# One block of rows fewer, and the last shared expert woven with the return of the routed rows

## The chip, the cores and the metric

The kernel runs on one core of a Trainium2 chip. The metric is the device time of one execution in microseconds (us). A core has five engines that run side by side, each with its own in-order stream of instructions: TensorE (PE, matrix products; its weight loads are shown as PEld), VectorE (DVE), ScalarE (ACT), GpSimd (POOL) and SyncE (SP, which only issues transfers here). Transfers between the device memory and the on-chip buffers run on 16 DMA engines and are issued by SP, ACT or POOL; an indirect transfer, whose rows are picked by a list of row numbers, is issued by POOL.

## The reference

The program is a two-layer decoder on 4 batches of 512 tokens with 512 features. Layer one has causal attention, cross attention and a ternary feed-forward network; layer two has attention, a learned adjacency and a mixture of experts. Only the last part is touched by the change:

```python
logits = flat @ router_w.T                       # 2048 tokens, 16 experts
scores = softmax(logits)
_, topk_idx = top_k(logits + router_bias, 2)     # two experts for each token
... # their scores, divided by the sum of the two, become combine[n, e]
for e in range(16):
    h = silu(flat @ Wu[e]) * (flat @ Wg[e])      # 512 -> 256
    out = out + combine[:, e:e+1] * (h @ Wd[e])  # 256 -> 512
out = out + silu(flat @ Su) * (flat @ Sg) @ Sd   # shared expert, 512 -> 512 -> 512
x = layernorm(x + out)
```

Each token so goes to two routed experts, and each token also goes through the shared expert.

## The kernel before, in words

All of it is in `experts`. The 4096 pairs of a token and an expert are sorted by expert into rows of a list `xs` in device memory, in blocks of 128 rows that belong to one expert each. Since each expert's last block may be partly empty, the list can need at most `NB = (2*B*S + NE*(P-1)) // P` blocks, which is 47. The blocks are worked on in three interleaved streams (`NS = 3`) of `LS = 16` blocks, and 3 x 16 is `NBP = 48`, so that the kernel before works on 48.

The order of the work, as the text has it:

1. POOL sends the rows of all 16 tiles of 128 tokens into `xs` (L1294, 32 indirect transfers, two for each tile).
2. `shared(b, acc[b])` is run for the batches 0, 1 and 2 while the rows travel. It goes through the shared expert in two halves of 256 hidden features. In each half, there are two products of `xT` with `swu` and `swg` (L1193, 8 matmuls for each of two groups of 128 features), a Silu on ACT (L1198), a multiplication on DVE into `sh` (L1199), and then two products with `swd` (L1204, 8 matmuls each), which DVE adds to the sum (L1210).
3. The 48 blocks. For each, SP loads the expert's weights where they differ from the last ones of its stream, and the 128 rows into `xb` (L1329). PE transposes them (L1334), DVE copies the result (L1336), PE multiplies (L1339, 8 matmuls), ACT and DVE make `h` (L1344, L1346), PE transposes `h` (L1349) and multiplies by `wd` (L1353, 4 matmuls), ACT copies the result into `yb` (L1358) and issues its store into the list `ys` in device memory (L1359). The tags `xb` and `yb` have three buffers each (`bufs=3` of the pool `hp`).
4. `shared(B - 1, acc[B - 1])`, the shared expert of the last batch.
5. The return. For each of 16 tiles of tokens, and each of its two experts, POOL gathers 128 rows of `ys` into a buffer `yg` (L1366), and DVE multiplies them by the token's weight and adds them to the sum (L1370). `yg` has four buffers of its own, which are called homes here. After the four tiles of a batch comes `layernorm(b, acc[b])`: statistics on DVE (L105, L106), a square root on ACT (L108), a reciprocal (L110) and four scalings on DVE (L112). Then SP stores the batch (L1375).

A gather needs every store into `ys` to have landed, since any row may lie in any block. The sum of the last batch (`acc[3]`, which is `X[3]`, shown as `x` in the profile) can take no routed rows before both halves of its shared expert have been added by L1210.

The text of the kernel is not the order in which an engine runs. The framework's planner lays down a fixed stream for each engine before anything runs: it simulates the program and gives an engine the earliest instruction of the text among those that are ready by its own estimate. In the trace, the statistics of batch 0 stand between multiplications of L1370 that the text has ahead of them, and L1199 of the last batch stands between multiplications that the text has behind it. On the chip, each stream is then kept to, even where the instruction at its head waits and the one behind it could run.

Of the kernel before, what the change touches and what calls it, by code (L numbers as in the profile page):

```python
# [13 lines left out]
F32 = mybir.dt.float32  # L14
# [7 lines left out]
P = 128  # L22
B, S, D = 4, 512, 512
# [17 lines left out]
def decoder_kernel(ctx: ExitStack, tc: tile.TileContext, a: dict, out: bass.AP):  # L41
# [16 lines left out]
    def psum_pair():  # L58
        return ps["sc"].tile([P, 2, 512], F32, tag="sc", name="sc")

    def psum_tp(dt=F32, n=4):
        return ps["tp"].tile([P, n, P], dt, tag="tp", name="tp")

    def psum_mm():
        return ps["mm"].tile([P, 512], F32, tag="mm", name="mm")
# [25 lines left out]
    for b in range(B):  # L91
        xb = const.tile([P, NT, D], F32, tag=f"x{b}", name=f"x{b}")
# [1002 lines left out]
    NB = (2 * B * S + NE * (P - 1)) // P  # L1095
    NS = 3
    LS = -(-NB // NS)
    NBP = NS * LS

    def experts(xs, ys):  # L1100
        with tc.tile_pool(name="mx", bufs=1) as xp:

            acc = [
                xp.tile([P, NT, D], F32, tag=f"acc{b}", name=f"acc{b}") for b in range(2)
            ] + X[2:]
# [78 lines left out]
            def shared(b, acc):  # L1184

                for half in range(2):
                    h = xp.tile([P, F // P, S], F32, tag="sh", name="sh", bufs=2)
                    for f in range(F // P):
                        col = ts(half * (F // P) + f, P)
                        pp = psum_pair()  # L1190
                        for j, w in enumerate((swu, swg)):
                            for c in range(NK):
                                T.matmul(  # L1193
                                    pp[:, j, :], w[:, c, col], xT[b][:, c, :],
                                    start=(c == 0), stop=(c == NK - 1),
                                )
                        s = xp.tile([P, S], F32, tag="ss", name="ss", bufs=2)
                        A.activation(s, pp[:, 0, :], AF.Silu)  # L1198
                        V.tensor_tensor(h[:, f, :], pp[:, 1, :], s, ALU.mult)  # L1199
                    for k in range(NT // 2):  # L1200
                        po = psum_pair()
                        for i in range(2):
                            for f in range(F // P):
                                T.matmul(  # L1204
                                    po[:, i, :], h[:, f, ts(2 * k + i, P)],
                                    swd[:, half * (F // P) + f, :],
                                    start=(f == 0), stop=(f == F // P - 1),
                                )
                        two = slice(2 * k, 2 * k + 2)
                        V.tensor_tensor(  # L1210
                            acc[:, two, :], po, (acc if half else X[b])[:, two, :], ALU.add
                        )

            with tc.tile_pool(name="sims3", bufs=1) as sp, tc.tile_pool(name="adj", bufs=2) as ap:
                sims = Similarities(sp)
# [6 lines left out]
                rest = sp.tile([P, 1], F32, tag="rest", name="rest")  # L1222
                V.tensor_scalar(rest, gam, -1.0, 2.0, ALU.mult, ALU.add)
                for b in range(B):
                    mix_adjacency(b, sims, ap, half, rest)
                    t = xp.tile([P, NK, S], F32, tag=f"xT{b}", name=f"xT{b}")
# [64 lines left out]
            for t in chain(range(2 * NT, TT), range(2 * NT)):  # L1291
                b, i = divmod(t, NT)
# [6 lines left out]
                        tc.declare_no_dep(d.ins, e.ins, reason="rows of their own")  # L1299
                    sent.append(d)  # L1300
            for b in range(3):
                shared(b, acc[b])

            with tc.tile_pool(name="mw", bufs=1) as wp, tc.tile_pool(name="mh", bufs=3) as hp:
                wug = [wp.tile([P, NK, 2, F], F32, tag=f"wug{s}", name=f"wug{s}") for s in range(NS)]
                wd = [wp.tile([P, F // P, D], F32, tag=f"wd{s}", name=f"wd{s}") for s in range(NS)]
                last = None
                for k in range(LS):
                    for s in range(NS):
                        j = s * LS + k  # L1310

                        with tc.issue_after(last.ins) if last else nullcontext():
                            e = nc.sync.value_load(ebi[0:1, j : j + 1], min_val=0, max_val=NE - 1)
                            kw = {}
                            if k:
                                kw["cond"] = nc.sync.value_load(
                                    newi[0:1, j : j + 1], min_val=0, max_val=1
                                )
                        for q, n in enumerate("ug"):
                            nc.sync.dma_start(  # L1320
                                wug[s][:, :, q, :],
                                a["W" + n][bass.ds(e, 1)].rearrange("o (c p) f -> p (o c) f", p=P),
                                **kw,
                            )
                        last = nc.sync.dma_start(
                            wd[s], a["Wd"][bass.ds(e, 1)].rearrange("o (c p) f -> p (o c) f", p=P), **kw
                        )
                        xb = hp.tile([P, D], F32, tag="xb", name="xb")
                        d = nc.sync.dma_start(xb, xs[ts(j, P), :])  # L1329
                        for e in sent:  # L1330
                            tc.add_manual_dep(d.ins, e.ins.name, SYNC, reason="all rows are there")
                        tp = psum_tp()
                        for c in range(NK):
                            T.transpose(tp[:, c, :], xb[:, ts(c, P)], ident)  # L1334
                        xbT = hp.tile([P, NK, P], F32, tag="xbT", name="xbT")
                        V.tensor_copy(xbT, tp)  # L1336
                        pp = psum_pair()
                        for c in range(NK):
                            T.matmul(  # L1339
                                pp[:, 0, :], xbT[:, c, :], wug[s][:, c, :, :].rearrange("p q f -> p (q f)"),  # L1340
                                start=(c == 0), stop=(c == NK - 1),
                            )
                        sl = hp.tile([P, F], F32, tag="sl", name="sl")
                        A.activation(sl, pp[:, 0, :F], AF.Silu)  # L1344
                        h = hp.tile([P, F], F32, tag="h", name="h")
                        V.tensor_tensor(h, pp[:, 0, F:], sl, ALU.mult)  # L1346
                        th = psum_mm()
                        for c in range(F // P):
                            T.transpose(th[:, ts(c, P)], h[:, ts(c, P)], ident)  # L1349
                        hT = hp.tile([P, F // P, P], F32, tag="hT", name="hT")  # L1350
                        A.copy(hT, th[:, :F].rearrange("p (c t) -> p c t", t=P))
                        for c in range(F // P):
                            T.matmul(  # L1353
                                pp[:, 1, :], hT[:, c, :], wd[s][:, c, :],
                                start=(c == 0), stop=(c == F // P - 1),
                            )
                        yb = hp.tile([P, D], F32, tag="yb", name="yb")
                        A.copy(yb, pp[:, 1, :])  # L1358
                        nc.scalar.dma_start(ys[ts(j, P), :], yb)  # L1359
                shared(B - 1, acc[B - 1])  # L1360
                for b in range(B):
                    for i in range(NT):
                        t = b * NT + i
                        for k in range(2):
                            y = hp.tile([P, D], F32, tag="yg", name="yg", bufs=4)
                            G.indirect_dma_start(  # L1366
                                out=y, out_offset=None, in_=ys,
                                in_offset=bass.IndirectOffsetOnAxis(pos[k][:, t : t + 1], 0),
                            )
                            V.scalar_tensor_tensor(  # L1370
                                acc[b][:, i, :], y, wt[k][:, t : t + 1], acc[b][:, i, :],
                                ALU.mult, ALU.add,
                            )
                    layernorm(b, acc[b])
                    nc.sync.dma_start(out[b].rearrange("(t p) d -> p t d", p=P), acc[b])  # L1375

    xs = tc.dram_tile([NBP * P, D], F32, name="xs")
    ys = tc.dram_tile([NBP * P, D], F32, name="ys")


    def selecting(batches, pool, before=()):
# [43 lines left out]
    with psum(2, 2, 2):  # L1425
        experts(xs, ys)
# [47 lines left out]
```

## Time and profile before

| what | us |
|---|---|
| median of 3 runs | 2590.51 (2584.24 to 2602.18) |
| profiled execution, its own time | 2586.26 |
| span of that execution, first to last instruction | 2584.5 |
| first expert product of the blocks (L1339) on the chain | at 2189.58 |
| issue of the last store into `ys` (L1359) | at 2511.56 |
| first and last issue of a gather (L1366) | at 2514.38 and 2570.67 |
| issue of the last batch's store (L1375) | at 2579.1 |

The columns of the page's groups are: line, engine, operation, output and inputs, count, then the busy time and the mean of one in ns, then how long the engine sat idle just ahead of them and what ended most of that. PE's mean in such a group is longer than its pace, since its matmuls overlap. Over the whole program, PE is busy for 88% of the span, DVE for 56%, ACT for 44%, POOL for 24%. These shares say little for the change, which touches the last 75 us alone: from 2514.4 to the end, a stretch of 70.10 us, PE is busy for 38.97 us, DVE for 48.79, ACT for 9.99 and POOL for 33.35.

### The profile page before, as it was taken

To read this page: it belongs to the slowest core of one execution; us is meant where nothing else is said; L and a number is where in the kernel's file an instruction comes from. 1 tells how busy PE (TensorE), PEld (TensorE's weight loads), DVE (VectorE), ACT (ScalarE), POOL (GpSimd) and SP (SyncE) were. 2 spreads that over 40 slices of the span, in tenths; PEclk is the share of its full clock that TensorE was granted. 3 is DMA by queue.
4 is the path that set the end of the run, shared out by engine and by line. 5 is a ranking of instruction groups with operands and counts; after the bars stand their busy time and mean duration, and the time that the engine had idled before them with its cause. 6 is when DMAs were issued, how large, how long until landed. Compare 5 with 4: busy or idle time off the path is not lost. (4 is left out here: it accounts for less than half of the span.)

```text
span 2584.5 us, 34904 instructions
## 1 busy us (share of the span) xinstructions
PE 2284.4 (88%) x13080; PEld 1010.3 (39%) x13080; DVE 1437.7 (56%) x3146; ACT 1128.1 (44%) x1770; POOL 624.9 (24%) x1218
## 2 busy tenths in 40 slices
PE   6899999979899899998995899989985999999995
PEld 2334333423333333355553334434342334444442
DVE  2455455567878788578886355545554672111117
ACT  0632462326777677656663443282331430221211
POOL 7300120033334233066674310040000004000004
PEclk9999999889999999999998999989987999999997
DMA  6500000072412210000001100000001006534535
GB/s 217 149 22 1 1 1 1 1 265 94 130 34 91 74 34 17 1 1 1 1 1 32 52 1 1 1 1 1 1 3 58 9 1 231 164 106 157 173 118 183
DMA packets 89884, 156.93 MB, mean 61 GB/s; under 512 B 7152, under 2 KB 39280, under 8 KB 89712
## 3 DMA queue, kind: packets, MB, share of 16 engines
q1 hardware_dynamic: 72304, 115.86, 13.9%
q10 hardware_dynamic: 12288, 22.03, 2.3%
q0 software_dynamic: 5120, 16.78, 2.0%
q8 instruction: 103, 1.69, 0.3%
q14 instruction: 69, 0.57, 0.1%
HBM read 161.99 MB, written 47.71 MB: 81 GB/s over the span
## 5 line engine op out<-in xcount | busy, mean ns | idle before, releaser
L552 DVE TENSOR_REDUCE nm<-sc 128x2 f32<-128x1024 f32 x256 | 304.2, 1218 | 99.7 <-PE sc L422 99.1
L590 ACT ACTIVATE p<-sc 128x1024 f32<-128x1024 f32 x256 | 248.5, 1024 | 135.3 <-PE sc L422 135.3
L246 DVE CUSTOM_DVE_ANT_0 e<-sc,late_keys 128x256 bf16<-128x256 f32 (+3 forms) x512 | 222.8, 484 | 130.9 <-PE sc L422 130.7
L296 ACT ACTIVATE p<-sc 128x512 f32<-128x512 f32 (+3 forms) x256 | 165.9, 700 | 234.1 <-PE sc L422 233.9
L422 PE MATMUL mm<-p,va 128*32 128x512 f32 (+3 forms) x2048 | 217.4, 529 | 0.4 <-ACT oT L605 0.3
L1339 PE MATMUL sc<-wug,xbT 128*128 128x512 f32 x384 | 185.9, 600 | 12.8 <-issue 7.0
L422 PE MATMUL sc<-qs,ks 128*128 128x512 bf16 x512 | 149.7, 384 | 29.3 <-DVE nm L552 28.1
L422 PE MATMUL sc<-ks,qs 128*128 128x512 bf16 x512 | 158.3, 394 | 1.8 <-DVE nm L552 1.6
L422 PE MATMUL sc<-kT,qT 32*128 32x512 f32 (+3 forms) x1024 | 128.8, 497 | 19.1 <-ACT p L296 15.7
L324 DVE RECIPROCAL u<-u 128x128 f32<-128x128 f32 x128 | 108.4, 909 | 64.6 <-ACT u L311 64.6
L422 PE MATMUL sc<-qT,kT 32*128 32x256 f32 (+3 forms) x1024 | 129.2, 504 | 14.4 <-DVE st L246 12.5
L998 ACT ACTIVATE junk<-sim,mid 128x512 bf16<-128x512 f32 x176 | 125.1, 724 | 16.3 <-POOL mid L991 16.3
L1366 POOL DMA_INDIRECT yg<-ys,pi x32 | 33.4, 1043 | 364.3 <-DMA ys<-yb 340.4
L743 POOL TENSOR_TENSOR y<-z 128x512 f32<-128x512 f32 (+1 forms) x48 | 97.4, 2041 | 87.3 <-DVE z L728 87.3
L1346 DVE TENSOR_TENSOR h<-sc,sl 128x256 f32<-128x256 f32 x48 | 20.2, 421 | 163.4 <-ACT sl L1344 163.4
L1339 PEld LDWEIGHTS sc<-wug,xbT 128*128 128x128 f32 x384 | 68.5, 192 | 82.4 <-issue 74.9
L743 POOL TENSOR_TENSOR z<-y 128x512 f32<-128x512 f32 x64 | 95.2, 1506 | 3.4 <-issue 2.1
L1353 PE MATMUL sc<-wd,hT 128*128 128x512 f32 x192 | 93.2, 609 | 0.0
L422 PEld LDWEIGHTS sc<-kT,qT 32*128 32x128 f32 x1024 | 49.7, 188 | 109.5 <-issue 74.1
L422 PEld LDWEIGHTS <-ks 128*128 128x128 bf16 x512 | 50.2, 99 | 108.1 <-issue 63.1
L1336 DVE COPY xbT<-tp 128x512 f32<-128x512 f32 x48 | 32.9, 685 | 104.6 <-PE tp L1334 104.6
L422 PEld LDWEIGHTS sc<-qT,kT 32*128 32x128 f32 x1024 | 50.4, 191 | 92.0 <-issue 62.0
(299 smaller groups left out, 4255.5 us busy)
## 6 DMA issues: line engine op xcount, KB each, us to landing
wug<-in_Wu SPq DMA_DIRECT2D x48, 512.0 KB
wug<-in_Wg SPq DMA_DIRECT2D x48, 512.0 KB
wd<-in_Wd SPq DMA_DIRECT2D x48, 512.0 KB
xs<-zero SPq DMA_DIRECT2D x3, 4096.0 KB
xb<-xs SPq DMA_DIRECT2D x48, 256.0 KB
ys<-yb ACTq DMA_DIRECT2D x48, 256.0 KB
w<-in_w_gate SPq DMA_DIRECT2D x16, 512.0 KB
w<-in_w_up SPq DMA_DIRECT2D x16, 512.0 KB
```

The lines of the kernel that those rows point to most:

```text
L246: V.tensor_tensor_reduce(e, at[r], late_keys[:, (NT - m) * P :], 1.0, LOWEST, ALU.add, ALU.max, accum_out=st[:, i, r : r + 1],)
L296: A.activation(heads, sc[h][:, :, :m], AF.Exp)
L324: V.reciprocal(sums[:, ts(i, P)], sums[:, ts(i, P)])
L422: ins = op(*args, **kw)
L552: V.tensor_reduce(NM[n][:, i, 2 * h : 2 * h + 2], sc, AX.X, ALU.max, negate=True)
L590: A.activation(p[:, 2 * h : 2 * h + 2, :], sc[h], AF.Exp)
L743: then(pool, getattr(G, op)(*args))
L998: A.activation(e, s[k], AF.Sign, bias=bias[:, k : k + 1], accum_out=to[:, k : k + 1])
L1336: V.tensor_copy(xbT, tp)
L1339: T.matmul(pp[:, 0, :], xbT[:, c, :], wug[s][:, c, :, :].rearrange("p q f -> p (q f)"), start=(c == 0), stop=(c == NK - 1),)
L1353: T.matmul(pp[:, 1, :], hT[:, c, :], wd[s][:, c, :], start=(c == 0), stop=(c == F // P - 1),)
L1366: G.indirect_dma_start(out=y, out_offset=None, in_=ys, in_offset=bass.IndirectOffsetOnAxis(pos[k][:, t : t + 1], 0),)
```

## The change

The last of the 48 blocks is skipped, with its weight loads, its rows and its store; `ys` shrinks to 47 blocks. `shared` becomes a generator that stops after each of its eight pieces (two hidden groups and two output pairs in each half). For the batches 0 to 2, it is run through at once, as before. For the last batch, it is started only with the return: one piece of it comes ahead of the gathers of each of the tiles 0, 1, 3, 4, 6, 7, 9 and 10, and what may be left comes ahead of batch 3. Last, the gathered rows go in turn into buffers of the tags `yg`, `xb` and `yb`, three of each, so that there are nine homes in place of four.

```diff
-                shared(b, acc[b])
+                for _ in shared(b, acc[b]):
+                    pass
...
                         j = s * LS + k
+                        if j == NB:
+                            continue
...
-                shared(B - 1, acc[B - 1])
+
+                rest = shared(B - 1, acc[B - 1])
                 for b in range(B):
+                    if b == B - 1:
+                        for _ in rest:
+                            pass
                     for i in range(NT):
                         t = b * NT + i
+                        if t % 3 != 2:
+                            next(rest, None)
                         for k in range(2):
-                            y = hp.tile([P, D], F32, tag="yg", name="yg", bufs=4)
+
+                            y = hp.tile([P, D], F32, tag=("yg", "xb", "yb")[(2 * t + k) % 3], name="yg")
                             G.indirect_dma_start(
...
-    ys = tc.dram_tile([NBP * P, D], F32, name="ys")
+    ys = tc.dram_tile([NB * P, D], F32, name="ys")
```

In `shared`, a `yield` is added behind L1199 (a hidden group) and behind L1210 (an output pair).

## The prediction

> **What bounds the kernel now.** I read the chain of work that ended last, cut to the final 80 us, then the waits of that stretch, then VectorE's instructions in order of time, and last the rows of the indirect transfers. The chain comes first, since it says which stage the change can shorten. Its columns are start, length and what.
>
> ```profile
> 2503.82 2.58 PE sc L1339 x6
> 2506.39 1.72 PE sc L1193 x4
> ...
> 2511.56 2.01 DMA ys<-yb
> ...
> 2514.38 2.24 DMA yg<-ys,pi
> ...
> 2552.64 5.38 DMA yg<-ys,pi
> ...
> 2558.06 5.77 issue
> ...
> 2570.67 3.62 DMA yg<-ys,pi
> ```
>
> Up to 2511 the chain is TensorE going from block to block; then it waits for the last store of a block, and from 2514 on it is gathers, with TensorE gone from it. The last block is so on the path in full, and behind it the path is the return. In the return, the waits are (total, times, longest):
>
> ```profile
> POOL yg L1366 <- DVE x L1370: 11.9, 5, 6.2
> POOL yg L1366 <- DVE acc L1370: 4.2, 5, 1.3
> PE sc L1204 <- DVE sh L1199: 11.8, 2, 7.6
> DVE acc L1370 <- DMA yg<-ys,pi: 6.2, 6, 1.5
> DVE x L1370 <- DMA yg<-ys,pi: 5.0, 6, 1.8
> ```
>
> POOL waits for VectorE to free a home, VectorE waits for gathered rows, and TensorE twice waits for a multiplication of the shared expert that stands in VectorE's stream behind multiplications of gathered rows. That third wait shows in VectorE's stream:
>
> ```profile
> 2515.86 0.69 DVE L1199 TENSOR_TENSOR sh<-sc,ss 128x512 f32<-128x512 f32 x1 [8.59 <-ACT ss L1198]
> ...
> 2526.43 0.67 DVE L1199 TENSOR_TENSOR sh<-sc,ss 128x512 f32<-128x512 f32 x1
> ...
> 2556.32 0.67 DVE L1199 TENSOR_TENSOR sh<-sc,ss 128x512 f32<-128x512 f32 x1
> ...
> 2565.69 1.21 DVE L1210 TENSOR_TENSOR x<-sc,x 128x1024 f32<-128x1024 f32 x1
> ...
> 2577.13 1.92 DVE L112 TENSOR_SCALAR x<-x,bmv,brs 128x512 f32<-128x512 f32 x4
> ```
>
> The second of these had its Silu at 2522.70 and ran at 2526.43; the fourth had it at 2550.58 and ran at 2556.32. The last addition of the shared expert ends at 2566.9, and only then can the gathered rows of batch 3 be added. Meanwhile the four homes are full, so POOL stands still from 2558 to 2564 (the "issue" of 5.77 on the chain), and three gathers are still to be issued at 2567.83 and later. VectorE is busy for 48.8 of the 63.2 us between 2515.86 and its end at 2579.05; the last store takes the 5.4 us from there to the end of the span.
>
> **The block that goes.** The stores of the last three blocks are issued here:
>
> ```profile
> 2497.51 0.33 ACTq L1359 DMA_DIRECT2D ys<-yb  x1
> ...
> 2504.47 0.33 ACTq L1359 DMA_DIRECT2D ys<-yb  x1
> ...
> 2511.56 0.33 ACTq L1359 DMA_DIRECT2D ys<-yb  x1
> ```
>
> One step is 6.96 us, and the last one, with matmuls of the shared expert between its own, is 7.09. With 47 blocks, the last store is issued one step earlier: 2497.51 + 7.09 = 2504.60, so **6.96 us** sooner. All that follows in the return is as much earlier: the first gather at 2507.42, the first L1199 at 2508.9. The block's loads on SP and its store on ACT have nothing behind them that is waited for, so they add nothing to this sum. That TensorE has less to do in the gaps of the last block is no loss: the shared expert's matmuls still stand behind it and fill them as they do now.
>
> **The nine homes.** The gather is the same operation into other buffers, so its row stands: 32 gathers, 33.4 us, mean 1.043 us, with 0.30 us between two that wait for nothing. At 1.343 us for a step, the 31 steps from the first issue to the last take 41.6 us; now they take 56.3 (2514.38 to 2570.67). The 14.7 us between are POOL's waits for homes. More than four gathers under way at once the return does not show. The nearest row is the sending of the rows, which has no homes to wait for:
>
> ```profile
> L1294 POOL DMA_INDIRECT xs<-x,pi x32: 956/960/1231, 2133.5 to 2173.0; - x32
> ```
>
> Those 32 transfers of the same size went out at a step of 1.265 us throughout and took 6.0 us (median) to land, where a gather takes 3.7 (3.2 to 5.5). So the transfers keep up with POOL, and many under way cost at most some 2.3 us more of landing, once, not for each. As buffers, the six new homes cost nothing: `xb` is free when the last block's rows have been transposed, and `yb` when its store has landed, which each gather waits for anyhow. Both ends for the pace: 1.265 us as in the sending, which gives 39.2 us, and the longest gather (1.307 + 0.30), which gives 49.8. I take 1.343, since it was measured in the return itself, beside VectorE's work.
>
> Here the Trainium skill speaks against the change. Its page "SBUF — State Buffer", section "SBUF: two separate sides", says that a VectorE copy or scaling in its two-port mode locks GpSimd out while the latter writes the descriptors of a transfer, and gives some 620 ns for such a transfer alone and 3100 ns overlapped. By that figure, an estimate, 16 gathers that each meet one of the 16 scalings of L112 would take 16 x 2.5 = 40 us more. The trace agrees in direction only: the shortest gather took 0.942 us, and all 32 together 33.4 - 32 x 0.942 = 3.3 us more than that, with the same 16 scalings in the same stretch.
>
> **VectorE becomes the bound.** Nothing is taken from its 48.8 us: 32 multiplications at 0.743, 16 statistics at 0.675, the scalings, the shared expert's eight operations. At 1.343 us a gather, POOL hands over 32 in 45 us with the landing, and VectorE needs 48.8. What can go is its idle time, 14.4 us now. By cause, from its rows: 3.35 us ahead of the first four or five gathered tiles (1.21, 0.85, 0.72, 0.57), which POOL's pace sets and which stay; 5.87 us for gathered rows in the middle (1.47, 1.38, 1.77, 0.61, 0.64), the price of four homes, which go; 2.65 us for TensorE's last output pairs at 2559, of which I keep half, since more gathered rows lie ready but batch 3 cannot use them; 1.98 us for the last gathers (1.04, 0.57, 0.37), which go, for with nine homes all eight gathers of batch 3 have been issued before its sum is ready; and 0.36 us for the root on ACT, which stays. That leaves 5.0 us. **The sum:** 2508.9 + 48.8 + 5.0 = 2562.7 for VectorE's end, 2568.1 with the store, against 2584.5: 16.4 us less, of which 7.0 is the block and 9.4 VectorE's idle time.
>
> **The weave** I cost at nothing by itself. In the old stream, L1199 and L1210 already stand between the multiplications, since the planner puts work in when it deems it ready. Giving the pieces later places in the text can only move them back. The text would put the eight pieces behind 0, 2, 6, 8, 12, 14, 18 and 20 gathered tiles; the trace has the four L1199 behind 0, 7, 18 and 24. At 3.7 + 1.343 us for each tile, TensorE's 41.2 us (96 matmuls of 0.43) would not be held up by those places. If that cover fails, TensorE's waits (11.8 us now) grow; that is the last rival below.
>
> The profiled execution took 2586.26 us, 1.76 more than its span. 16.4 us less is 2569.9. The median of the runs shown is 4.2 us above the profiled one, and by it the sum is 2574.1. I take the middle, **2572 us**.
>
> **The rivals.**
>
> *VectorE never idles.* 2508.9 + 48.8 + 5.4 = 2563.1, a gain of 21.4 us: 2564.9 by the profile, 2569.1 by the median. POOL gives the same floor: 2507.42 + 41.6 + 3.7 + 4.7 (last multiplication to last scaling) + 5.4 = 2562.8. For it: the surplus of gathered rows. Against it: batch 3 waits for its shared expert, and the stream is fixed by estimates that the chip has missed by 4 to 6 us at the two late L1199.
>
> *Only the block counts.* If the planner, given more rows in flight, leaves the fourth L1199 behind the 24th multiplication and L1210 where it is, the last addition comes at 2566.9 - 6.96 = 2559.9 and what follows stays: a gain of 7.0 us, 2579 to 2583.5. For it: the weave then does not do what it says, as the order by readiness hardly looks at the text. Against it: even so, three late gathers would no longer be late.
>
> *The weave holds TensorE up, and it is slower.* The place is the second L1199 (first half, second group): behind it, TensorE still has 4 pieces of 3.43 and 2 of 6.86 us, 27.4 us, and the last addition 2.4. If the stream puts it behind all 24 multiplications of the batches 0 to 2, which at POOL's pace are done at 2542, the shared expert ends at 2572, and eight multiplications, statistics and scalings (10 us) and the store make 2588: 3 us slower, 2590 to 2594. The case decides from about 20 multiplications ahead of that L1199; now there are 7. For it: one in-order stream, and later places in the text. Against it: its place in the text is behind 2.
>
> A further page bears on the stores: "DMA: Bandwidth & Descriptors", section "Issuing engines are not separate DMA queues", has transfers of all issuers share the 16 engines. The trace agrees in the return's gathers, which landed in up to 5.5 us beside the stores of a batch; its price is within the 2.3 us above.
>
> **Chances and range.** The forecast (a gain of 11 to 20 us) 0.55; VectorE nearly never idle 0.16; only the block 0.18; slower 0.11. The range takes in the floor by the profile and a gain of nothing by the median: **2560 to 2591**. A change under 1%, 26 us, is about what a measurement of this kernel cannot tell from none. Faster by more than that needs the full floor and a little more: 0.13. Slower by more than that needs the last rival far beyond its price: 0.07. Within 1%: 0.80.
>
> **What would show it.** L1339 with 376 matmuls, and the first gather near 2507. The step of L1366 near 1.34 us with little waiting for L1370. VectorE busy for 48 to 49 us between its first L1199 and its end, with some 5 us idle. The last L1210 between 2545 and 2556, and the eight multiplications of batch 3 in one row behind it. I am wrong if gathers slow down with nine homes, or if L1199 stands further back than now.

## The result and the profile after

| | before | after |
|---|---|---|
| median of 13 runs each, us | 2590.03 (2584.24 to 2602.18) | 2579.46 (2573.09 to 2585.92) |
| profiled execution, its own time | 2586.26 | 2573.09 |
| its span | 2584.5 | 2571.1 |
| issue of the last store into `ys` | 2511.56 | 2503.27 |
| the return: from that store to the end of the span | 72.94 | 67.83 |
| first and last issue of a gather, behind that store | 2.82 and 59.11 | 3.03 and 45.25 |
| L1199 of the last batch, behind that store | 4.30, 14.87, 36.05, 44.76 | 4.31, 15.77, 34.78, 42.16 |
| VectorE's end, behind that store | 67.49 | 62.21 |

The ratio is 0.9952, with a 95% interval of 0.9937 to 0.9967: 10.6 us by the medians, a gain of 0.5%. In the profiled executions it is 13.4 us of span. 8.3 of these were there when the last store was issued, and 5.1 came in the return. Of the 8.3, 1.14 was already there when the first product of the blocks started (the sending of the rows also began 1.1 us sooner), ahead of all that the change takes away; the other 7.15 came within the blocks, where 6.96 had been computed for the one that goes.

In the changed kernel L1204, L1210, L1339, L1366 and L1370 are L1205, L1211, L1344, L1378 and L1382, and the store into `ys` is L1364. First, the instructions of ACT's queue, in order of time, for the last three stores (start, length):

```profile
2489.22 0.33 ACTq L1364 DMA_DIRECT2D ys<-yb  x1
2496.18 0.33 ACTq L1364 DMA_DIRECT2D ys<-yb  x1
2503.27 0.33 ACTq L1364 DMA_DIRECT2D ys<-yb  x1
```

The steps are 6.96 and 7.09 us, as before. The page's groups of the blocks' first product and of the gathers:

```profile
L1344 PE MATMUL sc<-wug,xbT 128*128 128x512 f32 x376 | 182.5, 601 | 12.6 <-issue 6.8
...
L1378 POOL DMA_INDIRECT yg<-ys,pi x32 | 33.7, 1054 | 343.0 <-issue 340.5
```

376 matmuls are 47 blocks. A gather takes 1.054 us in the mean, 1.043 before. The waits of the return in the changed kernel (total, times, longest):

```profile
PE sc L1205 <- DVE sh L1199: 7.8, 2, 5.1
DVE acc L1382 <- DMA yg<-ys,pi: 5.9, 7, 1.5
DVE x L1211 <- PE sc L1205: 2.9, 2, 2.4
...
POOL yg L1378 <- DVE bmv L106: 0.9, 3, 0.3
...
POOL yg L1378 <- DVE x L1382: 0.6, 2, 0.3
DVE x L1382 <- DMA yg<-ys,pi: 0.5, 1, 0.5
```

POOL's 16.1 us of waiting for VectorE to free a home are gone; the step from gather to gather is 42.2 / 31 = 1.36 us, where it was 1.82. TensorE waits 7.8 us for L1199 instead of 11.8. But VectorE still waits 5.9 + 0.5 us for gathered rows. The last lines show where in VectorE's stream it stands:

```profile
2509.74 0.75 DVE L1382 SCALAR_TENSOR_TENSOR acc<-yg,wt,acc 128x512 f32<-128x512 f32 x1 [1.47 <-DMA yg<-ys,pi]
2511.26 0.75 DVE L1382 SCALAR_TENSOR_TENSOR acc<-yg,wt,acc 128x512 f32<-128x512 f32 x1 [0.77 <-DMA yg<-ys,pi]
...
2519.04 0.68 DVE L1199 TENSOR_TENSOR sh<-sc,ss 128x512 f32<-128x512 f32 x1
...
2524.08 0.75 DVE L1382 SCALAR_TENSOR_TENSOR acc<-yg,wt,acc 128x512 f32<-128x512 f32 x1 [1.30 <-DMA yg<-ys,pi]
...
2545.43 0.67 DVE L1199 TENSOR_TENSOR sh<-sc,ss 128x512 f32<-128x512 f32 x1
...
2550.65 1.22 DVE L1211 TENSOR_TENSOR x<-sc,x 128x1024 f32<-128x1024 f32 x1 [2.42 <-PE sc L1205]
...
2554.40 1.22 DVE L1211 TENSOR_TENSOR x<-sc,x 128x1024 f32<-128x1024 f32 x1
2555.53 4.06 DVE L1382 SCALAR_TENSOR_TENSOR x<-yg,wt,x 128x512 f32<-128x512 f32 x6
```

Up to 2524 it waits for rows ahead of most multiplications; later, but for one wait of 0.54 us, it waits for TensorE and, 0.36 us, for ACT's last root. The last addition of the shared expert ends at 2555.6 instead of 2566.9, and behind it six of the eight multiplications of batch 3 run in one row, since their rows are there. The chain that ended last has turned accordingly:

```profile
2503.27 2.00 DMA ys<-yb
...
2506.30 3.41 DMA yg<-ys,pi
...
2532.66 4.69 DMA yg<-ys,pi
...
2546.15 4.48 PE sc L1205 x6
...
2558.18 1.42 DVE x L1382 x2
...
2564.57 0.91 DVE x L112 x2
```

No gather stands on its last 33 us any more, where the last gather of before ended the chain but for VectorE's last work. It goes by VectorE and TensorE in turn.

### The profile page after: what moved, and what is told of

It reads as the page before. It is cut to its first block, busy times and chain, and to the rows that moved or that the text cites. A ratio compares the mean times of both kernels' runs of the same rounds, so it can differ in the third digit from the quotient of the medians.

```text
span 2571.1 us, 34835 instructions
## 1 busy us (share of the span) xinstructions
PE 2276.3 (89%) x13062; PEld 1005.8 (39%) x13062; DVE 1438.1 (56%) x3144; ACT 1127.1 (44%) x1767; POOL 625.3 (24%) x1218
## 5 line engine op out<-in xcount | busy, mean ns | idle before, releaser
L1344 PE MATMUL sc<-wug,xbT 128*128 128x512 f32 x376 | 182.5, 601 | 12.6 <-issue 6.8
L998 ACT ACTIVATE junk<-sim,mid 128x512 bf16<-128x512 f32 x176 | 125.0, 722 | 16.3 <-POOL mid L991 16.3
L1378 POOL DMA_INDIRECT yg<-ys,pi x32 | 33.7, 1054 | 343.0 <-issue 340.5
L1344 PEld LDWEIGHTS sc<-wug,xbT 128*128 128x128 f32 x376 | 67.2, 192 | 80.9 <-issue 73.4
```

The lines of the kernel that those rows point to most:

```text
L998: A.activation(e, s[k], AF.Sign, bias=bias[:, k : k + 1], accum_out=to[:, k : k + 1])
L1344: T.matmul(pp[:, 0, :], xbT[:, c, :], wug[s][:, c, :, :].rearrange("p q f -> p (q f)"), start=(c == 0), stop=(c == NK - 1),)
```

## The experiments

The change has three parts: the block, the homes and the weave. They were run alone and in pairs, then a few more kernels on what turned up. The table has all runs beside the two of the prediction. "Return" is from the issue of the last store into `ys` to the end of the span, in the profiled execution. "Silu late" needs a word, because it will matter: it is how long ACT starts (L1198 or the table load ahead of it) after the end of the last matmul of L1193 that it needs, for the third and the fourth group of the last batch. The first two were never late, and on time is 0.04 to 0.10 us. Each ratio is against the kernel before on the same chip.

| kernel | blocks | homes | weave | return, us | Silu late, us | ratio (95% interval) |
|---|---|---|---|---|---|---|
| before, first measurement | 48 | 4 | no | 72.94 | – | 1 |
| after, first measurement | 47 | 9 | yes | 67.83 | – | 0.9952 (0.9937 to 0.9967) |
| e1_block, chip A | 47 | 4 | no | 72.92 | – | 0.9982 (0.9968 to 0.9996) |
| e2_homes, A | 48 | 9 | no | 76.10 | 8.57 | 1.0007 (0.9994 to 1.0020) |
| e3_weave, A | 48 | 4 | yes | 72.58 | – | 1.0005 (0.9996 to 1.0015) |
| e4_block_homes, A | 47 | 9 | no | 76.94 | 9.26 | 0.9989 (0.9974 to 1.0003) |
| r_after, chip B | 47 | 9 | yes | 70.50 | 0.56, 2.97 | 0.9975 (0.9958 to 0.9991) |
| r_e4, B | 47 | 9 | no | 76.96 | 9.26 | 0.9980 (0.9964 to 0.9995) |
| e6_cap, B | 47 | 9 | yes | 70.33 | 2.97 | 0.9973 (0.9954 to 0.9993) |
| e7_early, B | 47 | 9 | yes, L1199 sooner | 71.64 | 9.43, 7.00 | 0.9968 (0.9950 to 0.9986) |
| e8_send3, chip C | 47 | 9 | yes | 77.07 | 9.76 | 0.9983 (0.9963 to 1.0003) |
| e9_probe, C | 47 | 9 | yes | 77.75 | 10.82 | 0.9982 (0.9967 to 0.9996) |
| e10_six, C | 47 | 6 | yes | 70.70 | – | 0.9975 (0.9961 to 0.9988) |
| e5_block_weave, C | 47 | 4 | yes | 73.11 | – | 0.9974 (0.9958 to 0.9990) |

The chips A, B and C run the kernel before in 2611.53, 2612.09 and 2609.75 us, 20 to 22 us longer than the first measurement. The section on the hardware comes back to that.

### The block alone

```diff
                         j = s * LS + k
+                        if j == NB:
+                            continue
...
-    ys = tc.dram_tile([NBP * P, D], F32, name="ys")
+    ys = tc.dram_tile([NB * P, D], F32, name="ys")
```

> The kernel before with the 48th block skipped, and nothing else of the change. The measure is the return: from the issue of the last store into ys to the end of the span, 72.9 us in the profiled kernel before and 67.8 in the changed one. My theory (the block is worth its step of 6.96 us, all on the path): the return stays at 72.9 +- 0.7, and the time falls by 7 us (ratio 0.997). Rival (the block's share is hidden, since the shared expert's matmuls only move up): the return grows by what the block saves, to about 78, and the time falls by 0 to 2 us.

The return is 72.92 us, where the kernel before has 72.94, and the L1199 of the last batch stand at 4.31, 14.98, 35.8 and 44.49 behind the store, within 0.3 us of before. So the block is worth its step upstream of the return and nothing in it. From the first product of the blocks to the last store, the two kernels of chip A with 47 blocks take 314.98 and 314.96 us, the two with 48 take 321.88 and 322.01: 6.9 to 7.05 us. 7 of 2611.53 is a ratio of 0.9973, within the interval measured. Its return has the same waits as before:

```profile
PE sc L1204 <- DVE sh L1199: 11.6, 2, 7.2
POOL yg L1368 <- DVE x L1372: 11.5, 5, 6.3
```

### The homes alone, and the block with the homes

```diff
-                            y = hp.tile([P, D], F32, tag="yg", name="yg", bufs=4)
+                            y = hp.tile([P, D], F32, tag=("yg", "xb", "yb")[(2 * t + k) % 3], name="yg")
```

e4_block_homes has this edit and that of the block; r_e4 is the same kernel again on chip B.

> The kernel before with nine homes for the gathered rows in place of four, 48 blocks and no weave. Theory (homes): POOL's steps fall from 1.82 to 1.36 us and the return from 72.9 to 67.8 +- 0.7 us; the time falls by 5 us (ratio 0.998). Rival (weave): the return stays at 72.9, since VectorE's stream still has the shared expert behind gathered rows, and POOL's earlier gathers only wait longer to be added.

> The whole change but the weave: 47 blocks and nine homes, the last shared expert in one piece ahead of the return in the text. Theory (homes and block): as the changed kernel, return 67.8 +- 0.7 us and a ratio of 0.995. Rival (weave): return 72.9 and a ratio of 0.997.

> 47 blocks, nine homes, no weave, once more. Theory A (the chip): the same return as the changed kernel's beside it, within 1.5 us. Theory B (the weave): 76 to 77 us again, against 67.8 with the weave.

Here the theory met something that it had not in its list. The homes do what they should: no wait of POOL for a home, all gathers issued by 45 us behind the store (59 with four homes). But the return became longer: 76.10, 76.94 and 76.96 us, 3 to 4 us more than with four homes. The waits in the return of e4_block_homes:

```profile
PE sc L1204 <- DVE sh L1199: 16.0, 2, 11.1
...
ACT L1198 <- remote: 12.5, 1, 12.5
```

TensorE's longest wait for L1199 went from 7.2 to 11.1 us, and this L1199 does not wait its turn behind multiplications: VectorE is ready and waits for the Silu, and ACT starts the Silu 9.26 us after the matmuls that it needs have ended. The profile names no engine of the core that releases ACT ("remote"). The ratios of the three runs (1.0007, 0.9989, 0.9980) are in line with 3 to 4 us lost, and in the last two a block gained, but by themselves would not show it.

### The weave alone, and with the block

e3_weave has the generator and its eight calls, as in the diff of the change, with 48 blocks and four homes. e5_block_weave adds the edit of the block.

> The kernel before with the weave alone: 48 blocks, four homes. Theory (homes): the weave hardly moves anything, return 72.9 +- 0.7 us, time unchanged (ratio 1.000). Rival (weave): the shared expert's pieces come at better places and the return falls to 67.8. A third case, that the weave hurts with four homes: return 75 or more.

> 47 blocks and the weave, with the four homes of the kernel before. Theory (the weave does nothing where four homes set the pace, the block is worth 7.0 us upstream of the return): return 72.3 to 73.0 us, no late Silu in it, L1199 near 4.3, 14.9, 36 and 44.5 us behind the last store, a time 3 to 7 us below the kernel before, as with the block alone (ratio 0.998). Rival (the weave is worth something with the block): a return of 70.5 or less.

72.58 us against 72.94 before, and 73.11 against 72.92 with the block alone (on another chip): the weave is worth nothing that shows with four homes. VectorE's stream shows why. The planner puts the four L1199 behind 0, 6, 18 and 24 multiplications of gathered rows in before, and in e1, e3 and e5 just so. The homes move one of them by one: 0, 7, 18, 24 in the changed kernel, and the same in e2_homes and e4_block_homes, which have no weave. (The prediction has 0, 7, 18, 24 for the kernel before; its second L1199 stands behind 6. That was a miscount.)

With nine homes, r_after (70.50) against r_e4 (76.96) looked like 6.5 us for the weave. It is not the weave. e8_send3 has the same streams as r_after in the return, weave included, and took 77.07. The next two parts show what differed.

The streams settle what the weave can do with nine homes. From the last store on, TensorE, ACT and POOL have the same instructions in the same order in e4_block_homes and in the changed kernel, and VectorE's 92 differ in one place: the second addition of the shared expert (L1211) and the last scaling of batch 0 (L112, 0.5 us) change places.

### The changed kernel again, and with a limit on the sending

e6_cap names fewer of the sendings of rows as independent of each other, and e8_send3 makes each sending wait for the third one before it:

```diff
 # e6_cap
-                    for e in sent:
+                    for e in sent[-3:]:
...
 # e8_send3
+                    if len(sent) > 2:
+                        tc.add_manual_dep(d.ins, sent[-3].ins.name, SYNC, reason="three at a time")
                     sent.append(d)
```

> The changed kernel once more, beside a second run of 47 blocks with nine homes and no weave. With nine homes and no weave the profile had the fourth Silu of the shared expert (L1198) start 9.4 us after TensorE's last matmul for it, and in the sending of the rows two Silus 5 and 18 us late, none of which the profiled kernel before or the changed one had. Theory A (the chip): on that chip a signal from TensorE to ACT comes late while POOL keeps many indirect transfers under way; here all kernels show it or none does, and where it shows, the changed kernel's return is 75 to 78 us like that of the one without the weave. Theory B (the weave): the weave keeps the last Silu clear of the gathers; the return is 67.8 +- 1 us whatever the chip.

> The changed kernel with the sending of the rows held to four transfers under way: each waits for the landing of the fourth before it. Theory A (TensorE's signals are late while many indirect transfers are under way): on a chip that shows the late Silus, the two of the sending go and the time falls by 10 to 18 us; on one that does not, the sending takes 40 to 50 us in place of 39 and the time rises by 0 to 8 us. If the late Silus have nothing to do with the transfers under way, they stay where they were.

> The changed kernel, but each sending of rows (L1294) also waits for the landing of the third one before it, so that at most three are under way. On the chips of the experiments two Silus of batch 0's or 1's shared expert start 5.3 and 18.1 us late beside the sending, and TensorE stands for 18.55 us. Theory (a dense row of indirect transfers holds them back): at three under way and 4 to 6 us to land, the step grows from 1.265 to 1.4 to 2.0 us, the sending takes 45 to 64 us instead of 40.5, both Silus start less than 1 us late, and the blocks start some 18 us sooner, or as much sooner as the slower sending lets them: a time 10 to 18 us below the changed kernel's. Rival (the Silus are late whatever the density, until the sending is over): the second Silu is released 3 to 5 us behind the last packet, so 25 to 40 us late, and the time is 5 to 20 us above the changed kernel's. Should the step stay at 1.265, the run tells nothing.

Neither limit did anything to the sending: the 32 transfers still go out at a step of 1.265 us, in e6_cap because POOL's stream came out the same, in e8_send3 without a single wait of POOL between two sendings in the trace. So both say nothing on a slower sending, and are three runs of the changed kernel, counting r_after. Their returns are 70.50, 70.33 and 77.07 us, with the fourth Silu 2.97, 2.97 and 9.76 us late. The stream of POOL tells the first two from the third. In r_after, POOL's instructions and VectorE's, in order of time:

```profile
2573.17 1.09 POOL L1378 DMA_INDIRECT yg<-ys,pi  x1 [0.30 <-issue]
2574.57 3.50 POOL L1378 DMA_INDIRECT yg<-ys,pi  x1 [0.30 <-issue]
2578.37 0.95 POOL L1378 DMA_INDIRECT yg<-ys,pi  x1 [0.31 <-issue]
```

```profile
2574.51 2.73 DVE L1382 SCALAR_TENSOR_TENSOR x<-yg,wt,x 128x512 f32<-128x512 f32 x4
```

One gather took 3.50 us instead of about 1, and the Silu that TensorE's matmuls of 2574.5 had made possible started at 2577.5, while this gather was held up. In e6_cap the same gather took 3.50 us, from 2572.16, with the same result. In e8_send3 all gathers took under 1.4 us, at gaps of 0.30, up to the last one, and ACT started only behind them:

```profile
2571.54 0.94 POOL L1380 DMA_INDIRECT yg<-ys,pi  x1 [0.30 <-issue]
```

```profile
2575.50 1.28 ACT L1198 ACT_TABLE_LOAD   x1 [13.04 <-remote]
```

The first line is the last gather of e8_send3 (L1380 in its text), the second its fourth Silu. The last packet of its gathers ended at 2575.4. In e4_block_homes and r_e4 the fourth Silu came at 2580.49 and 2582.5 and the last packet ended at 2581.0 and 2582.6; in e9_probe at 2580.6 and 2580.3; in e2_homes at 2587.3 and 2588.4. So where POOL's gathers followed each other without a break, the fourth Silu started within 1.2 us of the end of the last one's packets, in five runs of five.

### One L1199 sooner

VectorE's second L1199 is made to come ahead of the fifth gathered tile:

```diff
+                next(rest)
+                early = next(rest)
                 for b in range(B):
...
-                            V.scalar_tensor_tensor(
+                            m = V.scalar_tensor_tensor(
...
+                            if t > 1 and b < B - 1:
+                                tc.add_manual_dep(m.ins, early.ins.name, ORDER, reason="early")
```

> The changed kernel with one order forced: VectorE's second multiplication of the shared expert (L1199) stands ahead of the fifth gathered tile in place of behind the seventh. Theory (the shared expert's chain through TensorE sets the end of the return): its stall of 5.2 us at L1205 falls to about 1.3, the last addition comes 4 us sooner and the return falls from 67.8 to 64 us. Rival (VectorE is the bound, as I predicted): its 48 us of work and the waits for rows stay, and the return falls by under 1.5 us.

The L1199 did come sooner: at 12.32 us behind the store, where r_after has 15.72, and TensorE had the third pair of products done at 2558.4. The gain was lost one step on, at the third Silu:

```profile
2567.86 1.28 ACT L1198 ACT_TABLE_LOAD   x1 [14.95 <-remote]
```

It started 9.43 us after its matmuls, 0.03 us ahead of the end of the last gather before a break of POOL's (2567.9 to 2572.1). The fourth, whose own matmuls were done at 2565.3, could only follow it and the root of L108, at 2572.30. The return is 71.64 us, 1.1 to 1.3 longer than those of r_after and e6_cap. That a shared piece that stands sooner in VectorE's stream shortens the return where the Silus are on time is neither shown nor excluded by this run.

### Six homes

If dense gathers are what makes a Silu late, six homes should be as good as nine on these chips. VectorE's, TensorE's and ACT's streams of this kernel are the changed kernel's, instruction by instruction; the homes alone differ.

```diff
-                            y = hp.tile([P, D], F32, tag=("yg", "xb", "yb")[(2 * t + k) % 3], name="yg")
+                            y = hp.tile([P, D], F32, tag=("yg", "xb")[k], name="yg")
```

> The changed kernel with six homes (yg and xb in turn) in place of nine; VectorE's and TensorE's streams are the same. Theory (the Silus of the return start late where gathers follow each other without a pause): POOL waits for homes again from about the eighth gather on, the step is 1.5 to 1.7 us, the fourth Silu starts less than 0.5 us late in place of 2.97, and the return is 68 to 70.5 us, as short as with nine homes (70.3 to 70.5) or shorter. Rival (gathered rows in store count and the late Silus don't): VectorE waits for gathered rows, and the return is 71 to 73 us, towards the 72.6 with four homes.

```profile
ACT L1198 <- PE sc L1193: 15.8, 2, 12.5
...
POOL yg L1378 <- DVE x L1382: 6.8, 2, 4.0
```

POOL waits for homes again (6.8 us, 4.0 at the longest), the step is 52.7 / 31 = 1.70 us, and the third and the fourth Silu of the last batch start 0.08 us after their matmuls, released by PE. The return is 70.70 us: 2.4 less than with four homes on the same chip (e5_block_weave, 73.11) and 6.4 less than with nine (e8_send3, 77.07). It is 0.2 us above what the theory had given and below the rival's 71, so the size alone would not decide; the Silus do. It is one profiled execution of each; the ratios of the three kernels (0.9975, 0.9974, 0.9983) do not tell them apart.

### A second reader of the same products

VectorE copies one column of the products that the Silu reads, to see who else is late:

```diff
                         A.activation(s, pp[:, 0, :], AF.Silu)
+                        r = xp.tile([P, 4], F32, tag="prr", name="prr", bufs=2)
+                        V.tensor_copy(r[:, 0:1], pp[:, 1, 0:1])
                         V.tensor_tensor(h[:, f, :], pp[:, 1, :], s, ALU.mult)
```

> The changed kernel with one more instruction in each piece of the shared expert: VectorE copies one column of the same two products (128 x 1, out of the same pair of accumulators) that the Silu reads, directly ahead of its multiplication L1199. In the sending VectorE has nothing else to do there. If TensorE's products or the message that they are done come late to everybody, the copy starts as late as the Silu, 5.3 and 18.1 us behind the end of the last matmul. If ScalarE alone is late (its own instructions, its own queue), the copy starts within 0.3 us of the end of the last matmul and the Silu 5.3 and 18.1 us behind it. The time is within 3 us of the changed kernel's either way.

The two late Silus beside the sending and one on time, as VectorE's instructions in order of time show the copy:

```profile
2170.74 0.16 DVE L1200 COPY prr<-sc 128x1 f32<-128x1 f32 x1 [14.62 <-issue]
...
2187.74 0.16 DVE L1200 COPY prr<-sc 128x1 f32<-128x1 f32 x1 [16.25 <-ACT ss L1198]
...
2204.62 0.16 DVE L1200 COPY prr<-sc 128x1 f32<-128x1 f32 x1 [6.32 <-ACT ss L1198]
```

The copies start 0.04, 0.03 and 0.03 us after the end of the Silu (it starts at 2170.10, 2187.11 and 2203.99 and takes 0.60), the on-time one too. So in this kernel the copy always waits for the Silu, and the probe decides nothing. It would need a second reader that the Silu does not hold back.

## Why the prediction was right, and where it was wrong

The time of 2579.46 us lies in the range of 2560 to 2591, 7.5 us above the number, and the change is under 1%, as said. By itself this shows little, since the range also takes in a gain of nothing. The forecast case, a gain of 11 to 20 us, was just missed by the medians (10.6 us; the interval gives 8.5 to 16.3) and met by the profiled pair: 13.4 us of span, where the sum had 16.4. Of the 13.4, the 1.14 us that were there ahead of the blocks are luck.

**The block: right.** 6.96 us were computed. 7.15 us came within the blocks in the two traces of the first measurement, 6.9 to 7.05 on chip A, and e1_block's return is that of before.

**The pace of the gathers: right.** 1.343 us were taken, 1.36 measured, the last gather issued 45.25 us behind the store. (The sending's 31 steps took 39.5 us, 1.27 in the mean; 1.265 is the usual one.) The first gather was seen at 2506.30 (2507 forecast), 376 matmuls of L1339, POOL's waits for L1370 gone, the last L1210 at 2554.40 to 2555.6 (2545 to 2556 forecast). The prediction's two signs of being wrong showed a trace of themselves and decided nothing: the mean gather went from 1.043 to 1.054 us, and the second L1199 stands behind one multiplication more, 0.9 us later behind the store.

**VectorE's idle time: the term that was mis-sized.** Its work was right (48.8 forecast, 48.2 measured), its idle time not: 5.0 us were kept, 9.7 measured, 9.65 of it in waits of over 0.15 us. That is the whole miss of the return: VectorE's end was put at 4.3 + 48.8 + 5.0 = 58.1 us behind the last store, and came at 62.21. Two parts of the 4.65:

- Waits for gathered rows, 6.4 us instead of 3.35. The prediction kept those ahead of the first tiles and let all later ones go, since POOL needs 45 us for all gathers and VectorE 48.8. But VectorE's work is not spread evenly. At the start it has only a multiplication of 0.75 us a tile and a statistic of 0.68 for every second tile, some 1.1 us, and is faster than POOL's 1.36; the first five waits are 1.47, 0.77, 0.75, 0.73 and 0.61, and three more follow, of 0.23, 1.30 and 0.54. The surplus of rows builds up only later. "VectorE becomes the bound" holds from about 2524 on.
- Waits for TensorE's last output pairs, 2.9 us instead of the 1.3 kept. The shared expert still ends last: the fourth L1199 moved only 2.6 us nearer to the store (44.76 to 42.16).

What was said to go with the last gathers (1.98 us) did go. In the profiled span the miss of 4.1 us at VectorE's end shows as 3.0 only, mainly since the last store came 1.3 us sooner than computed.

**The weave at nothing: right** (72.58 against 72.94; 73.11 against 72.92 with four homes), for the reason given: the planner hardly looks at the text. With nine homes it moves one addition by one place. So the 5.1 us of the return in the first measurement belong to the homes, with the order that comes with them. That is argued from the streams and not measured there, where neither part was run alone; six homes against four on chip C, with no late Silu in either return, gave 2.4 us.

**The rivals.** "Only the block counts" would have been 7.0 us; on the chips B and C the changed kernel's ratios are those of just that (r_after, e6_cap and e8_send3: 0.9975, 0.9973, 0.9983, against 0.9973 for 7 us). In the first measurement it gained 5.1 us more in the return, and the interval of 0.9937 to 0.9967 leaves 0.9973 out. "VectorE never idles" fell with 9.7 us of idle time. "The weave holds TensorE up" did not happen: its L1199 never moved back by more than one tile, and TensorE's wait for it went down from 11.8 to 7.8 us.

**The Trainium skill's page on the SBUF.** The prediction put an estimate of 40 us from the Trainium skill's page "SBUF — State Buffer", section "SBUF: two separate sides", beside the sum. The mean gather grew from 1.043 to 1.054 us, 0.4 us for all 32, so by the size the trace disagrees. Gathers that began within a multiplication of VectorE's did take longer, as the last section shows.

## What to carry to other kernels

When a wait for buffers goes, do not set the consumer's idle time to what its total of work leaves: lay the producer's step beside the consumer's work tile by tile, since a consumer that is the bound over the whole stretch can still starve in its first third. A part of a change that only reorders the text can come to almost nothing where a planner orders by readiness (one addition moved by one place here); read the planned order before giving it a price. And a removed pause can have been doing something: here, on three chips, ScalarE was late in the return only where nine homes had taken POOL's pauses away.

## What the runs showed of the hardware that was not expected

**ScalarE started late beside dense indirect transfers.** In the first measurement no Silu of the kernel before or the changed one was more than 0.10 us late, beside the sending or in the return. In all twelve runs on the chips A, B and C, two Silus beside the sending were late, the first by 3.3 to 10.5 us, the second by 18.1 to 18.6. TensorE then stood still, and it is on the path there. Its instructions in order of time, from r_after and then from the kernel before in the first measurement:

```profile
2170.32 1.08 PE L1205 MATMUL sc<-swd,sh 128*128 128x512 f32 x2
2189.94 9.05 PE L1205 MATMUL sc<-swd,sh 128*128 128x512 f32 x14 [18.55 <-DVE sh L1199]
```

```profile
2160.31 1.02 PE L1204 MATMUL sc<-swd,sh 128*128 128x512 f32 x2
2161.88 6.28 PE L1204 MATMUL sc<-swd,sh 128*128 128x512 f32 x14 [0.55 <-DVE sh L1199]
```

The wait is 18.0 us longer. The kernel before is 20 to 22 us slower on these chips than in the first measurement, and most of that would be this wait. There is no trace of the kernel before on them, but e3_weave has the same work up to the return: it takes 398.71 us from the first sending to the last store, where the kernel before took 378.05, and TensorE's wait in it is 18.74 us in place of 0.55. Its span is 23.5 us longer, so the wait is most of that.

In the return, the count by homes is plain: with four or six homes none of the late pair in four runs (e1, e3, e5, e10), with nine homes at least one in all eight, by 2.97 to 10.82 us. Where the gathers ran to their end without a break, ACT came with their last packets; where one gather was held up for 3.50 us, ACT came within it; in e7_early it came as a row of gathers ended, 2.4 us ahead of that row's last packet. Beside the sending, the first late Silu started while POOL went on at its step of 1.265 us; the second started 3.2 to 3.7 us behind the end of the sending's last packet, in all twelve runs.

The kept traces also hold the messages by which one engine releases another, the count-ups of semaphores. A Silu on time starts 0.02 to 0.08 us behind TensorE's message, which is recorded 0.01 to 0.02 us after the last matmul. 31 of the 33 late ones (without e7_early's fourth, which followed the third) also start 0.02 to 0.07 us behind a message of TensorE's; that message is the late part, and ACT answers it at once. What holds it back stays open. In these traces records are lost as well: of the 128 messages of each of the eight semaphores of the indirect transfers, the first measurement has all, the runs on A to C 31 to 86, and of TensorE's five messages beside the sending none is there at its time, though one of the five released its Silu within 0.10 us. So late messages and lost records come together, and no run here tells whether the recording has a part in the delay. It is also open why the first measurement had neither. The probe did not decide it, and a slower sending, which might be worth most of the 18 us on such chips, was not achieved.

**A gather takes longer when it begins within one of VectorE's multiplications.** Over the 14 traces, the 83 gathers that began while VectorE did nothing took 0.953 us in the mean, at most 0.99, and the 110 that began within an addition, a statistic or L1199 0.948. The 221 that began within a multiplication of a gathered row (SCALAR_TENSOR_TENSOR, L1370, 0.75 us) took 1.16, and the sooner within it, the longer: 1.17 in the mean for a start 0.3 to 0.5 us into it, 1.31 for 0.2 to 0.3, 1.41 for 0.1 to 0.2. It looks as if the gather waits for that multiplication's end and slips in ahead of the next one; no run was made on it. Nine began at most 0.06 us into one, and with these it goes either way: four took 0.94 to 0.95, two 1.50 to 1.52, and three missed the gap and were held up for a whole row of multiplications, 3.50, 3.50 and 2.83 us beside four, four and three of them. That is much like the lock that the prediction cites from the Trainium skill's page "SBUF — State Buffer", section "SBUF: two separate sides": 3.50 us measured beside its 3100 ns. But it came with these multiplications and hardly with the scalings that the prediction had looked at (32 gathers began within L112 alone, 1.02 in the mean and at most 1.205), and it went to such a length 3 times in 448 gathers, not 16 times in 32.
